# The last layer of a sixteen-batch perceiver moved into the attention in front of it, with three smaller edits

## The chip, the cores and the metric

The kernel runs on one core of one Trainium2 chip. The time is the device time of one execution in microseconds (us). A core has TensorE (PE; its weight loads are shown apart as PEld), VectorE (DVE), ScalarE (ACT), GpSimd (POOL) and SyncE (SP), which here issues all loads and stores. Each runs its own list of instructions in order; they meet through semaphores.

## The reference

Twelve sections run one after the other on x, a 16 x 64 x 256 array in float32: four layers, each with a cross-attention over a context of 16 x 1601 x 256, a self-attention and a feed-forward part. Each section adds its result to x after a layer norm of x. What matters here:

```
# layer 0, cross-attention (16 heads; k, v are the context): softmax over keys
attn = softmax(where(mask, min, q k^T / 4));  x += concat(attn v) w_o
# layer 2, cross-attention: relu(scores + bias)^2 on the unmasked keys,
# divided by its sum, times v;  x += (...) Wo^T
# layer 3, self-attention: softmax(q k^T / 4 + relative bias, causal), projection
# layer 3, feed-forward: one linear layer with 8-bit weights
xn = layernorm(x)
x_scale = max(abs(xn), axis=-1) / 127          # at least 1e-6 before the division
x_q = clip(round(xn / x_scale), -128, 127)
x += (x_q @ weight_q) * x_scale * weight_scale + bias
```

## The kernel before, in words

The 1024 tokens (16 batches of 64) are eight tiles of 128 (`NT = 8`), two batches to a tile; x stays in SBUF as `self.x`, 128 x 8 x 256, for the whole run. `run` calls the sections of `STAGES`; each opens its own pools of SBUF and PSUM, and its first instructions wait until the memory they reuse is free.

A layer that plans the order sits between the program text and the engines: instructions go to their engine in an order that it derives from its own costs, unless a section sets `self.pinned`. Then `mm` and `tr` (lines 2018 and 2023, which nearly all products and transposes share in the profile) keep TensorE's instructions in the order in which the program writes them.

**Setup** (line 57) loads three things on SP's queue: the constants `cst` (the identity among them), x in one transfer of 1 MB, and the small vectors `vecs`. The weights of the first section and the first context tiles `cT` follow. SP's transfers share eight semaphores in turn, so a transfer may wait for the landing of the one eight before it.

**The norm** (`layernorm`, line 122) takes statistics of all eight tiles on VectorE (lines 127, 128), one reciprocal root for all (`rstd`, line 112: VectorE, ScalarE's square root, VectorE) and then eight normalisations (line 131). `transpose` (line 135) turns pairs of tiles on TensorE into `xT`, and products such as `lin_t` (line 156) or `lin` (line 170) follow. Five sections used it: the cross-attentions of layers 0 and 2, the expert sections of layers 0 and 2, and the last feed-forward section.

**The streamed cross-attentions** of layers 0 and 2 (`stream`, line 1914) go through 16 batches of 13 chunks of 128 keys, two chunks at a time: keys and values are projected (`pk`), scores are taken by key (`sc`), ScalarE makes weights `e` of them, and `values` (line 1959) multiplies them with the values into `acc`. The sums of the weights are made elsewhere: `total` (line 1948) adds `e` of each chunk into `tot` on GpSimd (line 1957), and when a batch is done `finish_heads` (line 1862) multiplies `tot` with ones into the second half of `acc`, takes the reciprocal and writes the batch's columns of the heads. Then `lin` with `wo` projects the heads tile by tile and `add_to_x` (line 330) adds them to x.

**The self-attention of layer 3** (`token_attention`, line 2041) runs over tiles with the order of TensorE pinned. In step t: `scores(t)` (scores, bias and maximum on VectorE, subtraction of the maximum on GpSimd, line 2136, exponential on ScalarE), `values(t - 1)` (turn of the weights on TensorE, copies on ScalarE, products and sums into `acc`, reciprocal and product on VectorE, lines 2162 and 2163), `project(t - 2)` (product with `wo`, addition to x). The tile of scores `sc` has one buffer, `mm` has two, which turns and projections share.

**The feed-forward of layer 3** (`l3_ffn`, line 1820) then runs over all of x: norm, maximum (line 1833), scale, three instructions a tile for the rounding (lines 1842 to 1844, with the large constant `big`), transposes of the bf16 result, product with the weights, scaling (line 1856), bias on GpSimd (line 1857), addition to x (line 1858). `run` ends with one store of x (line 2212).

Of the kernel before, what the change touches and what calls it, by code (L numbers as in the profile page):

```python
# [19 lines left out]
P = 128  # L20
# [29 lines left out]
class Sections:  # L50
# [6 lines left out]
    def setup(self, ctx):  # L57
        nc, tc = self.nc, self.tc
        self.const = ctx.enter_context(tc.tile_pool(name="const", bufs=1))
        self.wp = ctx.enter_context(tc.tile_pool(name="weights", bufs=1))  # L60
        n = self.d["consts"].shape[1]
        self.cst = self.const.tile([P, n], F32, tag="cst", name="cst")
        nc.sync.dma_start(self.cst, self.d["consts"])
        self.x = self.const.tile([P, NT, D], F32, tag="x", name="x")
        nc.sync.dma_start(self.x, self.d["x"].rearrange("(t p) d -> p t d", p=P))
        n = self.d["vecs"].shape[1]
        self.vecs = self.const.tile([P, n], F32, tag="vecs", name="vecs")
        nc.sync.dma_start(self.vecs, self.d["vecs"])
        self.ident = self.c("ident")
        self.ss = self.const.tile([P, NT, NCH, 2], F32, tag="ss", name="ss")  # L70

# [49 lines left out]

    def layernorm(self, pool, src, dst, eps=1e-5):
        nc = self.nc
        mv = pool.tile([P, NT, 2], F32, tag="ln_mv", name="ln_mv")
        for t in range(NT):
            st = pool.tile([P, 6], F32, tag="ln_st", name="ln_st", bufs=3)
            nc.vector.bn_stats(st, src[:, t, :])
            nc.vector.bn_aggr(mv[:, t, :], st)
        r = self.rstd(pool, mv[:, :, 1], eps, "ln_r")
        for t in range(NT):  # L130
            nc.vector.tensor_scalar(
                dst[:, t, :], src[:, t, :], mv[:, t, 0:1], r[:, t : t + 1], ALU.subtract, ALU.mult
            )

    def transpose(self, ps, src, dst, scale=None, shift=None, tag="tr"):

# [47 lines left out]
    def l0_xattn(self):  # L184
        nc, tc, d = self.nc, self.tc, self.d
        with ExitStack() as ctx:
# [4 lines left out]
            wk = self.w2(d["L0_xattn_w_k"], "wk")  # L191
            wv = self.w2(d["L0_xattn_w_v"], "wv")
            wo = self.w2(d["L0_xattn_w_o"], "wo")
            xln = sb2.tile([P, NT, D], F32, tag="e", name="xln", bufs=3)
            xT = sb.tile([P, KC, T], F32, tag="xT", name="xT")
            qT = sb.tile([P, KC, T], F32, tag="qT", name="qT")
# [1585 lines left out]
    def l3_attn(self):  # L1782
        nc, tc, d = self.nc, self.tc, self.d
        with ExitStack() as ctx:
# [22 lines left out]
            for h in range(2):  # L1807
                o = slice(h * S, (h + 1) * S)
                for r in range(4):
                    keys = slice(16 * r, 16 * r + 16)  # L1810
                    of = pb[o, r, : 16 * H].rearrange("p (k g r h) -> p h g r k", g=2, r=4, h=2)[:, h]
                    for g in range(KC):
                        for j in range(2):
                            nc.vector.tensor_tensor(
                                bias[o, :, 2 * g + j, keys], of[:, g], above[o, :, keys].to_broadcast([S, 4, 16]), ALU.add)
            self.token_attention(sb, sb2, ps, w, wo, self.v("L3_attn_b_attn"), rows, 0.25, False, bias)

    def l3_ffn(self):
        nc, tc, d = self.nc, self.tc, self.d
        with ExitStack() as ctx:  # L1820
            sb = ctx.enter_context(tc.tile_pool(name="l3f", bufs=1))
            ps = ctx.enter_context(tc.tile_pool(name="l3f_ps", bufs=2, space=PSUM))
            w8 = sb.tile([P, KC, D // 4], I32, tag="w8i", name="w8i")
            nc.sync.dma_start(w8, d["L3_ffn_weight_q"].rearrange("(c p) n -> p c n", p=P))
            w = sb.tile([P, KC, D], BF16, tag="wb", name="wb")
            nc.vector.tensor_copy(w, w8.bitcast(mybir.dt.int8))
            rows = self.row(sb, "L3_ffn_weight_scale", "L3_ffn_bias")
            identb = sb.tile([P, P], BF16, tag="identb", name="identb")
            nc.vector.tensor_copy(identb, self.ident)
            xln = sb.tile([P, NT, D], F32, tag="xln", name="xln")  # L1830
            self.layernorm(sb, self.x, xln)
            am = sb.tile([P, NT], F32, tag="am", name="am")
            nc.vector.tensor_reduce(am, xln, AX.X, ALU.max, apply_absolute_value=True)
            xs = sb.tile([P, NT], F32, tag="xs", name="xs")
            nc.vector.tensor_scalar(xs, am, 1e-6, 1.0 / 127.0, ALU.max, ALU.mult)
            rx = sb.tile([P, NT], F32, tag="rx", name="rx")
            nc.vector.reciprocal(rx, xs)
            xq = sb.tile([P, NT, D], BF16, tag="xq", name="xq")
            big = 1.5 * 2.0**23
            for t in range(NT):  # L1840
                q = sb.tile([P, D], F32, tag="q", name="q", bufs=2)
                nc.vector.tensor_scalar(q, xln[:, t, :], rx[:, t : t + 1], big, ALU.mult, ALU.add)
                nc.vector.tensor_scalar(q, q, big, 127.0, ALU.subtract, ALU.min)
                nc.vector.tensor_scalar(xq[:, t, :], q, -128.0, None, ALU.max)
            xqT = sb.tile([P, KC, T], BF16, tag="xqT", name="xqT")
            for t in range(0, NT, 2):
                pt = ps.tile([P, KC, 2, P], BF16, tag="tr", name="trb")
                for c in range(KC):
                    for j in range(2):
                        nc.tensor.transpose(pt[:, c, j, :], xq[:, t + j, c * P : (c + 1) * P], identb)  # L1850
                for c in range(KC):
                    self.copy(xqT[:, c, t * P : (t + 2) * P], pt[:, c].rearrange("p j x -> p (j x)"))

            def evac(t, pm):
                y = sb.tile([P, D], F32, tag="y", name="y", bufs=2)
                nc.vector.scalar_tensor_tensor(y, pm, xs[:, t : t + 1], rows[:, 0:D], ALU.mult, ALU.mult)
                nc.gpsimd.tensor_tensor(y, y, rows[:, D : 2 * D], ALU.add)
                nc.vector.tensor_tensor(self.x[:, t, :], y, self.x[:, t, :], ALU.add)

            self.lin(ps, w, xqT, evac)  # L1860

    def finish_heads(self, sb2, hT, b, acc, totals, ones, eps=None):


        nc = self.nc
        for g in range(2):
            for j in range(4):
                self.mm(
                    acc[32 * j : 32 * j + 32, 2 + g, :], ones, totals[g][j], start=False, stop=True, skip_group_check=True
                )  # L1870
        rec = sb2.tile([P, 2, P], F32, tag="rec", name="rec")
        if eps is None:
            nc.vector.reciprocal(rec, acc[:, 2:4, :])
        else:
            nc.vector.tensor_scalar(rec, acc[:, 2:4, :], eps, None, ALU.add)
            nc.vector.reciprocal(rec, rec)
        half = sb2.tile([P, 2, 2, S], F32, tag="half", name="half")
        own = self.c("own2")
        for h in range(2):
            q = slice(h * S, (h + 1) * S)  # L1880
            nc.vector.scalar_tensor_tensor(
                half[:, h], acc[:, 0:2, q], own[:, h : h + 1], rec[:, :, q], ALU.mult, ALU.mult
            )
        nc.vector.tensor_tensor(hT[:, :, b * S : (b + 1) * S], half[:, 0], half[:, 1], ALU.add)
# [29 lines left out]
    def stream(self, ps, sb2, load, wk, wv, copy, weights, finish, extra=None):  # L1914
# [44 lines left out]
        def values(n):  # L1959
            x, c = xs[n // NCH], n % NCH  # L1960
            e = by_chunk(es[n // 2])[:, :, :, n % 2, :]
            if c == 0:
                x.acc = ps.tile([P, 4, P], F32, tag="acc", name="acc")
            total(x, c, e)
            w = min(P, SK - c * P)
            for g in range(2):
                for j in range(4):
                    self.mm(
                        x.acc[32 * j : 32 * j + 32, g, :], x.v[:w, c, (4 * g + j) * 32 : (4 * g + j + 1) * 32],
                        e[:w, j, 2 * g : 2 * g + 2, :], start=(c == 0 and g == 0), stop=(c == NCH - 1),  # L1970
                        skip_group_check=True,
                    )
# [65 lines left out]
                        junk, piece[:, c - lo, :], AF.Square, accum_out=self.ss[:, b // 2, c, b % 2 : b % 2 + 1])  # L2038
                    yield

    def token_attention(self, sb, sb2, ps, w, wo, bias_t, rows, scale, own_input, bias=None):

# [128 lines left out]
        for _ in linear(0):  # L2173
            pass
        rest = linear(1)
        es = {}
        for t in range(NT + 2):
            if t < NT:
                es[t] = scores(t)
            for _ in range((3, 3, 2, 2)[t] if t < 4 else 0):  # L2180
                next(rest)
            if t == 3:
                next(rest, None)
            if 0 < t <= NT:
                values(t - 1, es.pop(t - 1))
            if t > 1:
                project(t - 2)
        self.pinned = False

    def l3_load(self, t, kind):  # L2190
# [3 lines left out]
        for j in range(2):  # L2194
# [5 lines left out]
            else:  # L2200
# [1 line left out]
            self.loaded[kind, t, j] = x  # L2202

    STAGES = ["l0_xattn", "l0_attn", "l0_ffn", "l1_xattn", "l1_attn", "l1_ffn",
              "l2_xattn", "l2_attn", "l2_ffn", "l3_xattn", "l3_attn", "l3_ffn"]

    def run(self, stages):
        with ExitStack() as ctx:
            self.setup(ctx)
            for s in stages:  # L2210
                getattr(self, s)()
            self.nc.sync.dma_start(self.out.rearrange("(t p) d -> p t d", p=P), self.x)

# [138 lines left out]
```

## Time and profile before

| what | us |
|---|---|
| median of three runs | 3904.95 (3902.84 to 3907.98) |
| the profiled execution, its own time | 3893.54 |
| its span | 3891.7 |
| TensorE busy in the span | 3541.6 |
| VectorE busy in the span | 1994.1 |
| ScalarE busy in the span | 1402.5 |
| GpSimd busy in the span | 1339.2 |
| first transpose of TensorE starts at | 12.44 |
| first streamed attention's last projection ends at about | 873.7 |
| layer 2's streamed attention's last projection ends at about | 3130.8 |
| last feed-forward section, first instruction of its norm at | 3857.41 |
| store of x issued at | 3885.88 |

The profile is of one execution on the chip; all starts are counted from the start of its span. A line of the timeline gives the start, the length, the engine, the line of the kernel, the operation, what it writes and reads, and in brackets how long the engine had been idle and what ended that. A busy TensorE is not one at its full pace; the granted clock says how much of the pace it was given.

### The profile page before, as it was taken

Reading aid. Unit: us, or ns where it says so; the run is one execution under the profiler, and the core shown is the slowest. Engines: PE = TensorE matmul, PEld = TensorE weight load, DVE = VectorE, ACT = ScalarE, POOL = GpSimd, SP = SyncE. Lnnn points to the kernel's source line nnn. Section 1 sums busy time; section 2 is a strip of 40 time slices with the busy share of each in tenths; the row PEclk is TensorE's granted clock in tenths of the full one; section 3 lists DMA queues with packets and bytes.
Section 4 is the critical chain, followed back from the end, with each engine's and each line's share of the span. In section 5 each row is a group of like instructions: output and inputs, shape, how many; then the busy total and the mean of one; then the engine's idle time right before and its main releaser. Section 6 shows DMA issues by size and latency. Waiting matters only on the chain.

```text
span 3891.7 us, 70627 instructions
## 1 busy us (share of the span) xinstructions
PE 3541.6 (91%) x30986; PEld 2238.7 (58%) x30986; DVE 1994.1 (51%) x3623; ACT 1402.5 (36%) x1955; POOL 1339.2 (34%) x767
## 2 busy tenths in 40 slices
PE   8999999988899988999997899899999879999985
PEld 4555555555565555555554566567676646555453
DVE  4333334335454445565656564567776656333346
ACT  2333333336411111444432433266666622111212
POOL 1555555562221101243331110377777740000011
PEclk9999999998999979999998999999999989999987
DMA  3111111006300004323400000211111004111640
GB/s 122 37 37 37 37 37 37 19 21 211 125 28 30 22 17 147 105 98 114 141 20 23 22 1 6 90 54 37 54 37 54 2 10 166 35 41 30 258 182 16
DMA packets 97212, 248.83 MB, mean 64 GB/s; under 512 B 7764, under 2 KB 68831, under 8 KB 94728
## 3 DMA queue, kind: packets, MB, share of 16 engines
q1 hardware_dynamic: 96904, 244.31, 17.6%
q8 instruction: 243, 3.98, 0.4%
q14 instruction: 65, 0.53, 0.0%
HBM read 243.24 MB, written 1.05 MB: 63 GB/s over the span
## 4 chain that ended last, share of the span: by engine, by line
PE 56%; DVE 10%; ACT 3%; issue 2%; POOL 1%; DMA 1%; SPq 0%; DVEq 0%; POOLq 0%; ACTq 0%
PE pk L2018 8%; PE sc L2018 7%; PE lin L177 5%; PE pu L2018 3%; PE gate L1619 3%; PE up L1619 3%; PE acc L2018 3%; PE pc L1246 3%; PE lin L442 2%; PE prz L2018 2%; PE lin_t L432 2%; PE lin_t L164 2%; PE gelu_t L1156 2%; PE turn L2023 1%; PE lin L2018 1%
## 5 line engine op out<-in xcount | busy, mean ns | idle before, releaser
L1957 POOL TENSOR_TENSOR tot<-tot,e 128x1024 f32<-128x1024 f32 (+1 forms) x352 | 831.3, 2362 | 377.3 <-ACT e L304 251.1
L247 DVE TENSOR_REDUCE m<-sc 128x4 f32<-128x2048 f32 x96 | 220.1, 2292 | 271.8 <-PE sc L2018 270.7
L1386 DVE SCALAR_TENSOR_TENSOR e<-sc,row_L_xattn_nbias,free 128x2048 f32<-128x2048 f32 x104 | 244.3, 2349 | 123.6 <-PE sc L2018 116.2
L1388 ACT ACTIVATE e<-e 128x2048 f32<-128x2048 f32 x104 | 198.6, 1910 | 244.7 <-DVE e L1386 244.7
L304 ACT ACTIVATE e<-sc 128x2048 f32<-128x2048 f32 x104 | 195.2, 1877 | 240.7 <-PE sc L2018 235.7
L2018 PE MATMUL sc<-qb,kT 32*128 32x128 f32 x6656 | 246.4, 285 | 38.5 <-DVE m L261 12.4
L2018 PEld LDWEIGHTS sc<-qb,kT 32*128 32x128 f32 x6656 | 207.3, 188 | 84.2 <-issue 24.9
L2018 PE MATMUL acc<-e,v 128*32 128x128 f32 x6656 | 229.0, 279 | 8.8 <-ACT e L1389 8.8
L2018 PEld LDWEIGHTS acc<-e,v 128*32 128x32 f32 x6656 | 171.9, 111 | 109.8 <-issue 96.3
L2018 PE MATMUL pk<-cT,wk 128*128 128x512 f32 (+1 forms) x512 | 208.0, 534 | 3.6 <-DVE rows L277 3.6
L2018 PE MATMUL pk<-wv,cT 128*128 128x256 f32 x832 | 208.6, 393 | 0.0
L1389 ACT ACTIVATE e<-e 128x2048 f32<-128x2048 f32 x104 | 198.8, 1911 | 3.3
L2018 PE MATMUL pk<-cT,wkv 128*128 128x512 f32 (+1 forms) x512 | 196.3, 524 | 0.0
L2018 PE MATMUL pk<-wkv,cT 128*128 128x256 f32 x832 | 196.3, 386 | 0.0
L2018 PEld LDWEIGHTS pk<-wv,cT 128*128 128x128 f32 x832 | 149.2, 189 | 75.3 <-issue 57.2
L2018 PEld LDWEIGHTS pk<-wkv,cT 128*128 128x128 f32 x832 | 153.2, 190 | 28.4 <-issue 4.3
L791 POOL TENSOR_TENSOR e<-e,mx 128x512 f32<-128x512 f32 x96 | 81.6, 882 | 214.0 <-DVE mx L790 214.0
L1246 PE MATMUL pc<-ew,eh 128*128 128x256 f32 x640 | 155.1, 385 | 0.0
L2018 PE MATMUL sc<-kT,qb 32*128 32x512 f32 (+2 forms) x1536 | 139.3, 460 | 12.2 <-issue 1.0
L2018 PE MATMUL pu<-cn,e 128*64 128x257 f32 (+1 forms) x1248 | 143.0, 385 | 5.6 <-POOL e L801 5.6
L1623 ACT ACTIVATE g<-gate 128x512 f32<-128x512 f32 x68 | 40.6, 597 | 294.6 <-PE gate L1619 294.6
L2018 PE MATMUL sc<-cT,qT 128*64 128x512 f32 (+1 forms) x768 | 142.3, 519 | 1.9 <-DMA cT<-in_ctx_t 1.3
(476 smaller groups left out, 6371.9 us busy)
## 6 DMA issues: line engine op xcount, KB each, us to landing
cT<-in_ctx_t SPq DMA_DIRECT2D x128, 832.0 KB
cn<-in_ctx_n SPq DMA_DIRECT2D x32, 1664.0 KB
piece<-in_ctx_n SPq DMA_DIRECT2D x16, 896.0 KB
piece<-in_ctx_n SPq DMA_DIRECT2D x16, 768.0 KB
w<-in_L_attn_W SPq DMA_DIRECT2D x8, 1024.0 KB
w<-in_L_ffn_W SPq DMA_DIRECT2D x16, 256.0 KB
down<-in_L_ffn_w_down SPq DMA_DIRECT2D x16, 256.0 KB
gate<-in_L_ffn_w_gate SPq DMA_DIRECT2D x16, 256.0 KB
```

What stands on the lines that cost most here:

```text
L164: nc.tensor.matmul(pm, w[:, k, n * P : (n + 1) * P], xT[:, k, h * 512 : (h + 1) * 512], start=(k == 0), stop=(k == kc - 1),)
L177: nc.tensor.matmul(pm, xT[:, k, t * P : (t + 1) * P], w[:, k, :], start=(k == 0), stop=(k == kc - 1))
L247: nc.vector.tensor_reduce(x.m4[:, g, :, i], pm, AX.X, ALU.max)
L304: nc.scalar.activation(e, pm, AF.Exp, scale=0.25)
L791: pin(nc.gpsimd.tensor_tensor(p.e, p.e, p.mx.unsqueeze(2).to_broadcast(p.shape), ALU.subtract))
L1246: nc.tensor.matmul(pc[:, n, j, :], s.eh[i][:, c, tok], ew2[:, c, cols], start=False, stop=(c == 3))
L1386: nc.vector.scalar_tensor_tensor(e16, pm16, nb, free[:, at : at + P].unsqueeze(1).to_broadcast([P, 16, P]), ALU.add, ALU.mult)
L1388: nc.scalar.activation(e, e, AF.Relu)
L1389: nc.scalar.activation(e, e, AF.Square)
L1619: nc.tensor.matmul(pm[-1], w[:, k, n * P : (n + 1) * P], xT[:, k, tok], start=(k == 0), stop=(k == KC - 1))
L1957: nc.gpsimd.tensor_tensor(tot[:w], x.first if c == 1 else tot[:w], e[:w], ALU.add)
L2018: ins = self.nc.tensor.matmul(*args, **kw)
```

## The change

Four edits. Setup loads x by two tiles, with the constants behind the first load and the vectors behind the first section's weights. `layernorm` works on two tiles at a time, each pair with its own root. In `stream`, the last batch's chunks 7 to 12 no longer go through GpSimd: TensorE multiplies `e` itself with ones (`add_sums`) beside the products with the values. And `l3_ffn` is no section of its own: it returns an object whose parts `token_attention` calls. After `project` of tiles 1, 3, 5, 6 and 7, `prepare` normalises and quantises the tiles that have become ready; in later steps `turn` transposes one of them in front of the attention's `values`, and `product` follows behind it and stores the tile. The rounding takes two VectorE instructions and one of ScalarE, the bias is added to x beforehand on GpSimd, and the copies of the transposes are ScalarE's. TensorE's order stays pinned throughout.

```diff
         self.cst = self.const.tile([P, n], F32, tag="cst", name="cst")
-        nc.sync.dma_start(self.cst, self.d["consts"])
         self.x = self.const.tile([P, NT, D], F32, tag="x", name="x")
-        nc.sync.dma_start(self.x, self.d["x"].rearrange("(t p) d -> p t d", p=P))
+        for t in range(0, NT, 2):
+            nc.sync.dma_start(self.x[:, t : t + 2], self.d["x"][t * P : (t + 2) * P].rearrange("(t p) d -> p t d", p=P))
+            if t == 0:
+                nc.sync.dma_start(self.cst, self.d["consts"])
...
     def layernorm(self, pool, src, dst, eps=1e-5):
         nc = self.nc
-        mv = pool.tile([P, NT, 2], F32, tag="ln_mv", name="ln_mv")
-        for t in range(NT):
-            st = pool.tile([P, 6], F32, tag="ln_st", name="ln_st", bufs=3)
-            nc.vector.bn_stats(st, src[:, t, :])
-            nc.vector.bn_aggr(mv[:, t, :], st)
-        r = self.rstd(pool, mv[:, :, 1], eps, "ln_r")
...
+        for t0 in range(0, NT, 2):
+            mv = pool.tile([P, 2, 2], F32, tag="ln_mv", name="ln_mv", bufs=2)
+            for j in range(2):
+                st = pool.tile([P, 6], F32, tag="ln_st", name="ln_st", bufs=3)
+                nc.vector.bn_stats(st, src[:, t0 + j, :])
+                nc.vector.bn_aggr(mv[:, j, :], st)
+            r = self.rstd(pool, mv[:, :, 1], eps, f"ln_r{t0}")
...
+            groups = {1: [0, 1], 3: [2, 3], 5: [4, 5], 6: [6], 7: [7]}
+            def prepare(s, us):
...
+                r = self.rstd(sb2, mv[:, :n, 1], 1e-5, "f_r")
+                xln = sb2.tile([P, 2, D], F32, tag="f_x", name="f_x")
+                for j, t in enumerate(us):
+                    nc.vector.tensor_scalar(
+                        xln[:, j, :], self.x[:, t, :], mv[:, j, 0:1], r[:, j : j + 1], ALU.subtract, ALU.mult)
+                am = sb2.tile([P, 2], F32, tag="f_am", name="f_am")
+                nc.vector.tensor_reduce(am[:, :n], xln[:, :n], AX.X, ALU.max, apply_absolute_value=True)
...
+                for j, t in enumerate(us):
+                    q = sb2.tile([P, D], F32, tag="f_q", name="f_q")
+                    nc.vector.tensor_scalar(q, xln[:, j, :], rx[:, j : j + 1], big, ALU.mult, ALU.add)
+                    nc.vector.tensor_scalar(q, q, big + 127.0, big - 128.0, ALU.min, ALU.max)
+                    xq[t] = sb2.tile([P, D], BF16, tag="f_xq", name="f_xq", bufs=4)
+                    nc.scalar.activation(xq[t], q, AF.Identity, bias=less)
+                    nc.gpsimd.tensor_tensor(self.x[:, t, :], self.x[:, t, :], rows[:, D : 2 * D], ALU.add)
+                    xs[t] = sc[:, j : j + 1]
+            def turn(s, t):
+                pt = ps.tile([P, KC, P], BF16, tag="mm", name="trb", bufs=2, padded_shape=[P, KC, 512])
                 for c in range(KC):
+                    self.tr(pt[:, c, :], xq[t][:, c * P : (c + 1) * P], identb)
+                xq[t] = sb2.tile([P, KC, P], BF16, tag="f_qT", name="f_qT")
+                nc.scalar.copy(xq[t], pt)
+            def product(s, t):
+                pm = ps.tile([P, D], F32, tag="mm", name="f_lin", bufs=2, padded_shape=[P, 512])
...
+                y = sb2.tile([P, D], F32, tag="f_y", name="f_y")
+                nc.vector.scalar_tensor_tensor(y, pm, xs[t], rows[:, 0:D], ALU.mult, ALU.mult)
                 nc.vector.tensor_tensor(self.x[:, t, :], y, self.x[:, t, :], ALU.add)
+                nc.sync.dma_start(self.out[t * P : (t + 1) * P, :], self.x[:, t, :])
...
+    def add_sums(self, acc, weights, w):
+        for g in range(2):
             for j in range(4):
                 self.mm(
+                    acc[32 * j : 32 * j + 32, 2 + g, :], self.c("ones")[:w, :32], weights[g][j], start=False, stop=True,
+                    skip_group_check=True)
...
-            total(x, c, e)
             w = min(P, SK - c * P)
+            if x.b < B - 1 or c < 7:
+                total(x, c, e)
+            else:
+                self.add_sums(x.acc, [[e[:w, j, 2 * g : 2 * g + 2, :] for j in range(4)] for g in range(2)], w)
...
+            now = ready[:1]
+            for u in now:
+                then.turn(u)
             if 0 < t <= NT:
                 values(t - 1, es.pop(t - 1))
+            for u in now:
+                then.product(u)
+                ready.remove(u)
             if t > 1:
                 project(t - 2)
+                if then is not None and t - 2 in then.groups:
+                    us = then.groups[t - 2]
+                    then.prepare(us)
+                    ready += us
+        for u in ready:
+            then.turn(u)
+        for u in ready:
+            then.product(u)
...
-            self.nc.sync.dma_start(self.out.rearrange("(t p) d -> p t d", p=P), self.x)
```

## The prediction

> **What bounds the kernel now.** I read the page first: TensorE is busy for 91% of the span, so most of the time can only be moved by an edit that takes TensorE work away, and this change takes none (it adds some). What it can win lies where TensorE stands still.
>
> ```profile
> span 3891.7 us, 70627 instructions
> PE 3541.6 (91%) x30986; PEld 2238.7 (58%) x30986; DVE 1994.1 (51%) x3623; ACT 1402.5 (36%) x1955; POOL 1339.2 (34%) x767
> ```
>
> Then the timeline around each place that the diff touches (columns: start, length, engine, line, operation, shape; in brackets the idle time before and what ended it). First, the end of the first streamed attention:
>
> ```profile
> 843.59 21.77 POOL L1957 TENSOR_TENSOR tot<-tot,e 128x1024 f32<-128x1024 f32 x9
> 853.46 1.08 PE L2018 MATMUL acc<-e,v 128*32 128x128 f32 x32
> 865.42 1.08 PE L2018 MATMUL acc<-tot,cst 128*32 128x128 f32 x16 [9.82 <-POOL tot L1957]
> 874.79 0.17 DVE L117 TENSOR_SCALAR ln_r<-ln_mv 128x4 f32<-128x4 f32 x1
> ```
>
> The last product with values ends at 854.5, but GpSimd is nine sums of 2.4 us behind, and TensorE waits until 865.4. In the windows view the granted clock of 865.4 to 877 is 0.65, so the last projections run slowly too. Layer 2's streamed attention ends the same way, with a shorter wait:
>
> ```profile
> 3120.18 1.08 PE L2018 MATMUL acc<-e,v 128*32 128x128 f32 x32
> 3124.28 0.64 PE L2018 MATMUL acc<-tot,cst 128*32 128x128 f32 x16 [2.40 <-POOL tot L1957]
> 3128.71 2.08 PE L177 MATMUL lin<-wo,xT 128*128 128x256 f32 x4 [3.15 <-DVE xT L1884]
> ```
>
> At the start TensorE waits for the norm of all eight tiles, which waits for one load of x:
>
> ```profile
> 7.93 0.75 DVE L127 BATCH_NORM_STATS2 ln_st<-x 128x6 f32<-128x256 f32 x2 [2.86 <-DMA x<-in_x]
> 12.44 2.08 PE L143 MATMUL tr<-cst,xln 128*128 128x128 f32 x8 [12.44 <-DVE xln L131]
> 17.73 7.03 PE L164 MATMUL lin_t<-xT,wq 128*128 128x512 f32 x16
> ```
>
> At the end the chain of waits is VectorE after the attention's last product (3855.7): 34.4 us, of which VectorE is busy 24.0, then one store. Before it the loop over tiles takes about 5.7 us a tile, with VectorE busy 22.2 of 31.3 us in the windows view.
>
> ```profile
> 3829.43 1.90 POOL L2136 TENSOR_TENSOR e<-e,mx 128x1024 f32<-128x1024 f32 x1 [8.98 <-DVE mx L2135]
> 3829.59 1.76 DVE L2162 RECIPROCAL rec<-acc 128x256 f32<-128x256 f32 x1 [0.33 <-PE acc L2018]
> 3861.33 1.28 ACT L118 ACT_TABLE_LOAD   x1 [9.37 <-DVE ln_r L117]
> 3885.88 0.40 SPq L2212 DMA_DIRECT2D out<-x  x1
> ```
>
> **Part 1, sums by ones (first stream).** For the last batch's chunks 7 to 12 GpSimd loses six sums of 2.36 us; TensorE gets six times eight products of the form of acc<-e,v. That row is 229.0 us for 6656 records, two to a product, so a chunk costs 0.54 us and all six 3.3. In the loop of 3.44 us around 850 the new 1.08 us per pair of chunks takes the place of one projection (1.13), which moves behind. GpSimd then ends at about 865.4 - 6 x 2.42 = 850.9, so its part is no longer waited for. From 853.46: sums and products 2.1, GpSimd's part 0.54: 856.1. Seven projections follow; the first two are paced by their additions behind the 1.76 us reciprocal in VectorE's order (until about 860), the others at 1.13. The norm of the next layer's first half needs tiles up to 5 and is queued behind them: 863.8, against 874.79 now. After it come the additions of tiles 6 and 7, which the table load (1.28) about covers. I take 10.5 us. Bounds: 13.5 if the additions don't pace the projections, 3 if GpSimd is still behind.
>
> **Part 1, second such stream.** Products and sums end at 3119.4 + 2.2 = 3121.6, GpSimd's part at 3122.1, then 0.42 + 1.74 + 0.6 + 0.3 with gaps to 3125.45, the last projection 1.1 warm and its addition 0.4: 3127.0, against 3131.24 now: 4.2 us. Bounds 2 and 6.
>
> **Part 2, start.** x comes in four loads, the constants behind the first, the vectors behind the weights. Three loads more on SP's queue, each 0.4 to 0.5 us of issue; the context loads there also wait for earlier loads of the ring (cT waited 1.9 us for x). They come later by some 2 us, but the queue stays full (348 GB/s until 24.6), and TensorE now asks for cT after lin_t instead of at 14.3, so nothing waits. The last pair still lands near 7.9. The statistics of pair 3 wait for that load, and pair 2's normalisation is queued behind them; this and pair 3's remainder take VectorE about 3.8 us, and TensorE's last transposes end near 12.2; lin_t starts there instead of 17.7, but the two context products (1.85 + 1.02) that ran before it now come after: 12.2 + 7.0 + 1.7 = 21.0 against 24.59, if TensorE is warm. The first 3.5 us of work ran at half pace (eight transposes 2.08, later eight 1.04). Sparse transposes may leave it so: 1.7 less. I take 3.0; bounds 1.5 and 4.5.
>
> **Part 3, norms by two tiles elsewhere.** VectorE gets six small instructions more (0.17 and 0.20 each), but TensorE's first transpose comes earlier: 1378.92 to about 1376.9, and the half-clocked 11 us of work behind it pull the gate's end from 1390.7 to about 1388.5: 2.0. In layer 2's expert stage 3241.18 to about 3240.0: 1.0. In the streamed attention of that layer the table load stays in front: 0.7. Bounds together 1 and 6.
>
> **Part 4, last layer inside the attention.** Gone from the end: all of 3857.3 to 3891.7 but the last tile's part. What is left after the last projection's addition: two single-tile norms and quantisations interleaved, 18 VectorE instructions, 5.3 us by the rows (0.17 to 0.40 each); then ACT 0.37, transposes 0.35, copy 0.42, product 0.6, scaling and addition 1.35; then the store. The old store's issue to the end took 5.8, of which its 1.05 MB moved for 3.0 us; a tile's is an eighth: 3.2. In all 11.7, so 22.7 won.
>
> Against it, the loop. TensorE's order is fixed there, and a tile's transposes stand in front of the attention's own turn. They need the whole quantisation of a pair, and that starts only when the second tile's addition is done. Behind these transposes wait, on the same queue, the turn of the attention's tile, its acc, both projections and the next scores, and VectorE's reciprocal waits for acc. (The eight stores wait on SP's queue with nothing but stores behind them.) Take the pair (0, 1), from its addition at 3825.98: hT and statistics to 3826.75; e and mx of tile 4, ahead in VectorE's order, 2.65: 3829.4. Now GpSimd's subtraction of tile 4 starts, 1.9 us. Then root 0.8, two normalisations 0.67, maximum 0.6, small ones 0.44, q 0.62 and 0.28, ACT 0.4, transposes 0.35, turn 0.66, copies 1.2, acc 1.35.
>
> Here a rule speaks against the change. The row: normalisations of this kind take 1.38 for four, but
>
> ```profile
> 3606.46 1.38 DVE L1662 TENSOR_SCALAR xln<-x,ln_mv,ln_r 128x256 f32<-128x256 f32 x4
> 3608.15 2.34 POOL L1668 TENSOR_TENSOR x<-x,row_L_xattn_bv 128x1024 f32<-128x1024 f32 x1 [371.90 <-PE tr L2023]
> 3609.00 2.62 DVE L1662 TENSOR_SCALAR xln<-x,ln_mv,ln_r 128x256 f32<-128x256 f32 x4 [0.17 <-PE tr L2023]
> ```
>
> the second four stand until GpSimd's operation is over. The Trainium skill, "SBUF — State Buffer", "Who interferes with whom": such a VectorE instruction and a GpSimd one lock each other out for the whole instruction. So the normalisations wait until 3831.45, and the small ones behind GpSimd's two new additions of the bias (0.7 each, L1857). The reciprocal of tile 3 (3829.59) comes at about 3839.0: 9.5 late. The pair (2, 3) has a statistic between mx and its root, so the root itself is locked out: 12.2 more. The pair (4, 5) meets no subtraction: 7.4 more. Sum 29.1. Behind the last reciprocal (3853.22, 38.5 us before the end) there are then about 17.9. Net 29.1 - 20.6 = 8.5 us slower. Without the lock the same walk gives 23.7 - 21.3 = 2.4 slower; if the queueing on TensorE cost nothing and only VectorE's added 3.1 us a tile counted, against 9 us idle there, 11 faster. I take 7 slower, near the locked walk, as its row is in this trace; range -11 to +12.
>
> Table loads: four more. The trace shows 1.28 and the root 0.01 later; "ScalarE: Activation LUTs", "What ACT_TABLE_LOAD costs", gives 2.66 with its drain. By the trace all fall into idle time of ACT; by the page the third root would come 1 us later. I follow the trace: 0. The weights' loads move from 3857 to before the loop: their 0.64 us of casts fall into VectorE's idle time there.
>
> **Sum.** -10.5 - 4.2 - 3.0 - 2.0 - 1.0 - 0.7 + 7 = -14.4. The profiled run took 3893.54 (span 3891.7), so 3879.1 for it; the median of the three runs is 11.4 above it, so 3904.95 - 14.4 = 3890.5.
>
> **Rivals.**
> - The last layer hides well after all (-11): 3872.5. For it: ACT and GpSimd are idle enough; against: the fixed TensorE order. 0.2.
> - GpSimd still gates the first stream's end (gain 3 instead of 10.5): 3898. For: it is busy 14.1 of 14.6 us before 854.6; against: six sums are 14 us. 0.1.
> - The start gains nothing, as the context loads come later than 19 us: 3893.5. For: SP's queue waits for landings; against: 13 us is when the first landed. 0.1.
> - Slower: the transposes in TensorE's order, from a cost of 29 us in the loop beyond what the end saves, 12 to 13 a pair more than walked: it would take every one of the quantisation's VectorE instructions being locked out. 3915. 0.05.
>
> **How the numbers follow.** My forecast 0.55. 0.2% is 7.8 us, about what this measurement tells from no change. Faster: 0.55 + 0.2 + 0.1 and half of the second rival, less the forecast's upper edge: 0.85; same 0.11; slower 0.04. The range runs from the first rival to the second: 3873 to 3899.
>
> **What would show it.** Right: no wait for tot before the last acc<-tot; lin_t near 12; rec of tile 7 some 25 to 29 us later relative to the stage's start and the end some 18 us behind it; f_x or f_r of 1 to 2 us beside GpSimd. Wrong: a loop that still takes 6 us a tile, or a TensorE gap near 856.

## The result, and the profile after

| kernel | median us | range | runs |
|---|---|---|---|
| before | 3904.95 | 3901.50 to 3910.06 | 5 |
| changed | 3890.39 | 3883.65 to 3895.43 | 5 |

The ratio is 0.9966, with a 95% interval of 0.9952 to 0.9980: 13 us less, between 8 and 19. The forecast was 3890.5. So the total was met almost to the microsecond, but not because every term was right, as the stretches show.

The page of the changed kernel, first lines:

```profile
span 3893.4 us, 71039 instructions
PE 3559.3 (91%) x31163; PEld 2254.0 (58%) x31178; DVE 2001.7 (51%) x3655; ACT 1415.8 (36%) x1987; POOL 1311.5 (34%) x756
```

This profiled execution took 3895.43 us, 1.9 more than the profiled one of before (3893.54), although the medians differ by 14.6 the other way: executions of one kernel scatter by some 10 us to either side of their median, and the one profiled of before was among the fastest of its kernel. Subtracting one span from the other would therefore say "no gain". What can be compared is each stretch between two instructions that both kernels have: the difference of the two starts, followed through the trace, shows where time is won and lost. It also shows a difference that no forecast named. In layer 2's self-attention, from about 3190 us of the trace of before to its end at about 3230, no instruction differs, and yet the changed kernel takes 7 us more there. The windows view of the same work, before and then after (columns: window, its length, the busy time and count of the five engines, granted clock, DMA share, GB/s):

```profile
3192.30:3212.30 20.00, 16.83 (x271) 12.79 (x270) 11.32 (x20) 4.92 (x4) 9.57 (x2) 0.83 0.01 2
3212.30:3232.30 20.00, 18.46 (x396) 15.29 (x398) 18.91 (x33) 0.00 (x0) 1.16 (x1) 0.91 0.01 2
```

```profile
3180.00:3200.00 20.00, 17.16 (x175) 13.02 (x175) 8.30 (x14) 4.92 (x4) 5.33 (x1) 0.63 0.01 2
3200.00:3220.00 20.00, 19.25 (x346) 16.20 (x346) 15.10 (x25) 0.00 (x0) 5.39 (x2) 0.69 0.01 2
```

The granted clock is 0.83 and 0.91 in the one, 0.63 and 0.69 in the other, and in the same 40 us TensorE gets through 667 products there, 521 here. Every later trace of this study has this stretch 4.4 to 7.3 us longer than the one of before, among them a kernel with nothing but part 1 changed (5.8). The work that takes 22.0 us there from 3190 on, at a granted clock of 0.84, takes 27.5 to 28.7 us at 0.63 in all ten. It may belong to the execution, for the one that was traced of before was 11 us faster than the median. But that kernel was traced only once, and all ten other traces hold part 1, so no run here excludes that it follows from the change. The stretches below leave it out.

Now the places that were forecast. The end of the first streamed attention, in the timeline of the changed kernel (start, length, engine, line, operation, shape, and in brackets the idle time before):

```profile
840.04 12.12 POOL L1986 TENSOR_TENSOR tot<-tot,e 128x1024 f32<-128x1024 f32 x5
856.11 0.62 PE L2050 MATMUL acc<-e,v 65*32 65x128 f32 x16
856.55 0.62 PE L2050 MATMUL acc<-tot,cst 128*32 128x128 f32 x16
863.68 0.17 DVE L118 TENSOR_SCALAR ln_r<-ln_mv 128x4 f32<-128x4 f32 x1
```

GpSimd ends at 852.2, TensorE takes its part at 856.55 with no idle time in front (9.82 us before), and the next norm's root begins at 863.68; the forecast had 863.8.

The start, same view:

```profile
7.22 1.23 PE L145 MATMUL tr<-cst,xln 128*128 128x128 f32 x4 [7.22 <-DVE xln L133]
11.63 1.98 PE L145 MATMUL tr<-cst,xln 128*128 128x128 f32 x8 [1.44 <-ACT xT L111]
13.67 9.12 PE L166 MATMUL lin_t<-xT,wq 128*128 128x512 f32 x16
22.62 5.31 PE L2050 MATMUL pk<-cT,wk 128*128 128x512 f32 x12
27.86 1.14 PE L2050 MATMUL sc<-kT,qb 32*128 32x512 f32 x8
```

The first transpose comes 5.2 us earlier than before, but the first scores (27.86) only 0.26 us earlier: lin_t, 7.03 us before, now takes 9.12.

And the end. Before and after in the windows view, from the reciprocal of tile 2 to that of tile 7, and from there to the end:

```profile
3823.70:3853.20 29.50, 24.29 (x829) 18.70 (x829) 21.62 (x23) 9.69 (x14) 7.60 (x4) 0.97 0.01 3
3853.20:3891.70 38.50, 8.47 (x40) 4.76 (x40) 26.82 (x79) 2.88 (x6) 5.61 (x8) 0.58 0.12 37
```

```profile
3822.00:3878.20 56.20, 31.06 (x847) 24.09 (x848) 38.99 (x75) 20.30 (x32) 12.02 (x10) 0.71 0.04 12
3878.20:3893.40 15.20, 4.63 (x22) 2.18 (x20) 10.15 (x32) 2.42 (x7) 1.44 (x2) 0.72 0.10 35
```

The last reciprocal is 26.7 us later against tile 2's, the end stands 15.2 behind it instead of 38.5: 68.0 us have become 71.4. The timeline says what holds the loop:

```profile
3828.11 1.99 DVE L1852 TENSOR_SCALAR f_x<-x,f_mv,f_r 128x256 f32<-128x256 f32 x2
3832.16 0.49 DVE L1863 TENSOR_SCALAR f_q<-f_q 128x256 f32<-128x256 f32 x2
3833.05 0.40 PE L2055 MATMUL trb<-identb,f_xq 128*128 128x128 bf16 x2 [8.17 <-ACT f_xq L1865]
3833.24 1.92 PE L2055 MATMUL turn<-cst,e 128*128 128x128 f32 x8
3837.47 1.76 DVE L2195 RECIPROCAL rec<-acc 128x256 f32<-128x256 f32 x1 [4.82 <-PE acc L2050]
```

TensorE stands idle for 8.17 us in front of trb, although the weights for the turn behind it have been ready since 3830.7. VectorE, which could do the attention's reciprocal, then waits 4.82 us for acc. The same pattern comes again at 3854.81 and 3873.74.

The table collects the stretches. "Measured" is the mean over all traces of this study that have the part, less the mean over those that don't; for the ends of the two streams that is the one trace of before, and for the start the two kernels with products of zeros (see below) are left out. In times of the trace of before, the first six rows run from 0 to 28.1 us, 848 to 882, 1341 to 1388, 2440 to 2477, 3060 to 3150 and 3232 to 3252.

| stretch | forecast | measured | the traces, as differences from the one of before |
|---|---|---|---|
| start, to the first scores | -3.0 | -0.8 | -1.5 to +0.6 with, -0.4 to +0.9 without |
| end of the first stream | -10.5 | -11.3 | -11.0 to -11.5 in ten traces |
| norm of layer 0's experts | -2.0 | -2.5 | -2.1 to -3.1 with, -0.2 to 0 without |
| norm in layer 2's stream | -0.7 | +0.3 | +0.1 to +3.3 with, 0 to +1.9 without |
| end of layer 2's stream | -4.2 | -2.0 | -3.0 to -4.5 in six traces, -0.6 to +1.1 in four |
| norm of layer 2's experts | -1.0 | -0.4 | -0.1 to +0.7 with, 0 to +1.2 without |
| last layer (tile 2's reciprocal to the end) | +7 | +2.6 | in full: 71.1 to 71.5 with, 68.0 to 69.4 without |
| sum | -14.4 | -14.1 | |

If the longer self-attention of layer 2 (6 us in the mean) belonged to part 1, the sum would be about -8, at the edge of the measured 8 to 19.

### The profile page after: what moved, and what is told of

It reads as the page before. It is cut to its first block, busy times and chain, and to the rows that moved or that the text cites. A ratio compares the mean times of both kernels' runs of the same rounds, so it can differ in the third digit from the quotient of the medians.

```text
span 3893.4 us, 71039 instructions
## 1 busy us (share of the span) xinstructions
PE 3559.3 (91%) x31163; PEld 2254.0 (58%) x31178; DVE 2001.7 (51%) x3655; ACT 1415.8 (36%) x1987; POOL 1311.5 (34%) x756
## 4 chain that ended last, share of the span: by engine, by line
PE 55%; DVE 10%; ACT 3%; issue 2%; POOL 1%; DMA 1%; DVEq 0%; ACTq 0%; SPq 0%; POOLq 0%
PE pk L2050 9%; PE sc L2050 7%; PE lin L179 5%; PE pu L2050 3%; PE acc L2050 3%; PE gate L1622 3%; PE up L1622 3%; PE pc L1249 3%; PE prz L2050 2%; PE lin_t L166 2%; PE lin L445 2%; PE turn L2055 1%; PE gelu_t L1159 1%; PE lin_t L435 1%; PE lin L2050 1%
## 5 line engine op out<-in xcount | busy, mean ns | idle before, releaser
L1986 POOL TENSOR_TENSOR tot<-tot,e 128x1024 f32<-128x1024 f32 (+1 forms) x340 | 803.0, 2362 | 375.0 <-ACT e L307 252.2
```

The source lines that it names most:

```text
L1986: nc.gpsimd.tensor_tensor(tot[:w], x.first if c == 1 else tot[:w], e[:w], ALU.add)
```

## The experiments

Times in one group were taken on one chip, with the kernel before beside them (medians 3903.65, 3903.95 and 3903.76 in the three groups).

### First group: what each part is worth, and what the end waits for

The last layer put back into a section of its own, with `l3_ffn` as in the kernel before:

```diff
-                ..., rows, 0.25, False, bias, self.l3_ffn(sb, sb2, ps))
+                ..., rows, 0.25, False, bias)
-    def l3_ffn(self, sb, sb2, ps):
...
+    def l3_ffn(self):
...
-              "l2_xattn", "l2_attn", "l2_ffn", "l3_xattn", "l3_attn"]
+              "l2_xattn", "l2_attn", "l2_ffn", "l3_xattn", "l3_attn", "l3_ffn"]
```

> The changed kernel, but the last layer stands in its own section behind the attention as before, with its maximum over all tiles, three-instruction rounding and one store (its norm goes by two tiles, as the shared function now does). My theory (the move into the attention costs about 7 us, as TensorE's fixed order makes the attention wait for the quantisation): the last reciprocal of the attention comes some 27 us earlier and the end 38 us behind it instead of 15, so 3890.4 - 7 = about 3883 to 3887. The rival (the last layer hides well, and the gain comes from it): about 3901.

Measured: 3889.78 (3881.91 to 3894.12), ratio 0.9967 (0.9955 to 0.9979), above the 3883 to 3887 of my theory. The total is level with the changed kernel's 0.9966, and intervals of some 5 us to either side settle neither theory beyond saying that the gain doesn't come from this part, since 3901 is excluded. The stretch settles the sign: 30.9 us between the two reciprocals and 37.7 behind, 68.7 against 71.4. The move costs 2 to 3 us, not 7.

The turn one step later:

```diff
-            now = ready[:1]
+            now = [u for u in ready[:1] if t > since[u] + 1]
...
                     ready += us
+                    since.update((u, t) for u in us)
```

> The changed kernel, but a prepared tile is transposed one step later than now, so that TensorE no longer waits for the quantisation in front of the attention's own turn. My theory (most of the 26.7 us by which the last reciprocal comes late is this wait): the reciprocal of tile 3 comes at its old place, the last one 8 to 14 us late instead of 26.7, the end 15 to 17 behind it: about 3874 to 3879. The rival (VectorE's added work, 3 us a tile, and its lock-out by GpSimd are the price, wherever the transposes stand): the last reciprocal stays over 20 us late, 3884 or more.

Measured: 3888.79 (3885.98 to 3893.45), ratio 0.9966 (0.9954 to 0.9978). The time is where the rival had it (3884 or more); the last reciprocal, 18.0 us late, lies between the 8 to 14 of my theory and the rival's 20. The trace tells why:

```profile
3827.69 1.76 DVE L2195 RECIPROCAL rec<-acc 128x256 f32<-128x256 f32 x1 [0.25 <-PE acc L2050]
3835.40 0.40 PE L2055 MATMUL trb<-identb,f_xq 128*128 128x128 bf16 x2 [5.63 <-ACT f_xq L1865]
3841.61 1.76 DVE L2195 RECIPROCAL rec<-acc 128x256 f32<-128x256 f32 x1 [6.52 <-PE acc L2050]
```

Tile 3's reciprocal is back in its old place (5.8 us behind tile 2's), as expected. But VectorE now takes the reciprocal and the next tile's maximum first, the quantisation ends only at 3835.7, and the transposes wait for it all the same, with tile 4's turn behind them. The wait was shortened and moved by a tile, not removed: 47.5 us between the reciprocals, 66.3 to the end. My expectation forgot that a later place in TensorE's order also lets VectorE do the quantisation later.

TensorE kept busy at the start:

```diff
-                    nc.tensor.transpose(pt[:, c, j, :], src[:, t + j, c * P : (c + 1) * P], self.ident)
+                    ins = nc.tensor.transpose(pt[:, c, j, :], src[:, t + j, c * P : (c + 1) * P], self.ident)
+                    if warm:
+                        self.tc.keep_in_program_order(ins)
+            for _ in range(warm[2] if warm else 0):
+                self.tc.keep_in_program_order(
+                    nc.tensor.matmul(warm[0], warm[1][:, :P], warm[1], start=True, stop=True))
...
+            for _ in range(14):
+                self.tc.keep_in_program_order(
+                    nc.tensor.matmul(idle, warm[:, :P], warm, start=True, stop=True))
             self.layernorm(sb, self.x, xln)
-            self.transpose(ps, xln, xT, tag="acc")
+            self.transpose(ps, xln, xT, tag="acc", warm=(idle, warm, 6))
```

These transposes and the products of zeros also keep the program's order on TensorE.

> The changed kernel, with 14 products of zeros (bf16, 128x512, into an unused PSUM tile) on TensorE before the first transposes and 6 behind each pair of tiles; their result is not used. My theory (the start gained only 0.3 us instead of 3.0, because TensorE ran the transposes and the first part of lin_t at half pace: 9.12 us against 7.03 before): lin_t takes about 7.0, the context's products after it begin about 2 to 3 us earlier than 22.6, and the kernel gains 2 to 3 us: about 3888. The rival (the late end of the transposes, 13.6, is what counts, or the loads): lin_t still takes 9, or the products wait for cT and wk, gain under 0.5.

Measured: 3897.77 (3888.46 to 3901.87), ratio 0.9983 (0.9974 to 0.9991).

```profile
1.19 5.86 PE L218 MATMUL idle<-warm 128*128 128x512 bf16 x14 [1.19 <-DVE warm L214]
13.62 0.60 PE L145 MATMUL tr<-cst,xln 128*128 128x128 f32 x4
14.05 1.46 PE L150 MATMUL idle<-warm 128*128 128x512 bf16 x5
15.35 7.03 PE L171 MATMUL lin_t<-xT,wq 128*128 128x512 f32 x16
```

lin_t takes 7.03, so the half pace was the cause of its 9.12; but the products of zeros behind the last pair hold it back by 1.5 us, so that the first scores come 0.4 us earlier than in the changed kernel, not 2 to 3. The total is even above the changed kernel's. Behind the start VectorE, ScalarE and GpSimd have the same order in both, and the excess arises in stretches whose code is the same. I can't tell its cause, and it didn't come again with the smaller warming below.

Part 1 alone, on the kernel before:

```diff
-            total(x, c, e)
             w = min(P, SK - c * P)
+            if x.b < B - 1 or c < 7:
+                total(x, c, e)
+            else:
+                self.add_sums(x.acc, [[e[:w, j, 2 * g : 2 * g + 2, :] for j in range(4)] for g in range(2)], w)
```

> The kernel before with one part of the change alone: the last batch's chunks 7 to 12 summed on TensorE by ones, in both streams. My theory: the end of the first stream comes 10 to 12 us earlier, that of layer 2's stream 4 us, so 3904.95 - 15 = about 3890. The rival (GpSimd is still behind): an idle time of TensorE before acc<-tot is left, 3898 to 3902.

Measured: 3895.07 (3890.71 to 3899.77), ratio 0.9980 (0.9969 to 0.9992): 3 to 12 us faster, below what I expected.

```profile
855.74 0.62 PE L2024 MATMUL acc<-e,v 65*32 65x128 f32 x16
856.17 0.62 PE L2024 MATMUL acc<-tot,cst 128*32 128x128 f32 x16
863.30 0.17 DVE L117 TENSOR_SCALAR ln_r<-ln_mv 128x4 f32<-128x4 f32 x1
```

No idle time is left before acc<-tot, so GpSimd isn't behind, and the stretch gives 11.4 us in the first stream and 3.5 at the end of the second, together 14.9 as expected. The time of whole runs shows only a part of it: its interval ends at 12. What takes the rest isn't known. The longer self-attention of layer 2, 5.8 us in this trace too, would be of the right size.

### Second group: the turn behind the attention

The changed kernel again, as its companion:

> The changed kernel unaltered, beside the next two on one chip. Both theories: about 3890 in time, and the last layer's stretch (from layer 3's attention's first row load to the end) some 5 to 7 us longer than in the kernel before.

Measured: 3887.88 (3880.85 to 3895.13), ratio 0.9963 (0.9950 to 0.9975); 71.3 us from tile 2's reciprocal to the end. From the first row load of layer 3's attention to the end it takes 4.1 us longer than before, less than the 5 to 7 expected; in the first trace of the changed kernel it is 6.8, of which 3.4 lie in front of tile 2's reciprocal.

Then the order that the trace of the turn one step later asks for. Nothing of the last layer stands in front of the attention's work of a step:

```diff
-            now = ready[:1]
-            for u in now:
-                then.turn(u)
+            for u in turned:
+                then.product(u)
             if 0 < t <= NT:
                 values(t - 1, es.pop(t - 1))
-            for u in now:
-                then.product(u)
-                ready.remove(u)
             if t > 1:
                 project(t - 2)
+                turned = [u for u in ready[:1] if t > since[u] + 1]
+                for u in turned:
+                    then.turn(u)
+                    ready.remove(u)
...
+                    since.update((u, t) for u in us)
+        for u in turned:
+            then.product(u)
         for u in ready:
```

> The changed kernel, but in each step a prepared tile is transposed behind the attention's turn, products and projection, no sooner than two steps after its preparation, and its product with the weights follows in the next step. My theory (TensorE's fixed order is the price: in the changed kernel and in the one with the turn a step later, the attention waited at the transposes until the quantisation was done): from the reciprocal of tile 2 to that of tile 7 about 40 us instead of 56.2 (29.5 before), from there to the end about 17, so that the stretch from tile 2's reciprocal to the end is 55 to 60 instead of 71.4 (68.0 before): 3874 to 3879. The rival (VectorE's added work is the price, wherever the transposes stand): 65 or more for this stretch, 3885 or more.

Measured: 3875.47 (3866.93 to 3882.14), ratio 0.9930 (0.9912 to 0.9948), 12.4 us below its companion.

```profile
3827.48 0.73 DVE L1852 TENSOR_SCALAR f_x<-x,f_mv,f_r 128x256 f32<-128x256 f32 x2
3833.17 0.28 PE L2055 MATMUL trb<-identb,f_xq 128*128 128x128 bf16 x2 [0.72 <-ACT f_xq L1865]
3848.07 1.72 DVE L1882 TENSOR_TENSOR x<-f_y,x 128x256 f32<-128x256 f32 x1
```

```profile
3819.60:3858.60 39.00, 29.80 (x844) 22.70 (x844) 34.87 (x72) 19.36 (x30) 12.67 (x10) 0.85 0.04 13
3858.60:3874.50 15.90, 4.92 (x26) 2.52 (x24) 10.90 (x35) 3.78 (x11) 1.48 (x2) 0.71 0.12 41
```

trb now costs TensorE 0.72 us of waiting instead of 8.17. 39.0 us lie between the reciprocals and 15.9 behind, 54.9 together: 16.4 less than the changed kernel, 13.1 less than the kernel before. VectorE is busy 34.87 of the 39.0 us, so here it is near its bound; in the changed kernel it was busy 39.0 of 56.2. The rival, that VectorE's added work is the price wherever the transposes stand, has fallen: it gave 65 or more. To the end, VectorE's busy time fell too, from 49.1 to 45.8 us, as fewer of its instructions run beside GpSimd's (f_x takes 0.73 in the first line, not 1.99). So up to 3.4 of the 16.4 us may come from that.

Parts 2 and 3 undone: setup and `layernorm` as in the kernel before, all else as changed.

> The changed kernel with x loaded in one transfer behind the constants and all norms by eight tiles, as before (parts 2 and 3 undone). From the two traces: the start within 0.5 us of the changed kernel's, the expert section of layer 0 some 3 us later, of layer 2 1 us later, the streamed attention of layer 2 1 to 2 us earlier: together 2 to 3.5 us slower, 3893. My forecast on record had 6.7 for these parts; if that holds, 3897.

Measured: 3891.24 (3881.77 to 3902.95, 22 runs), ratio 0.9971 (0.9964 to 0.9979), 3.4 us above its companion. The intervals overlap, but the stretches of parts 2 and 3 give 0.8 + 2.6 = 3.4 as well: the two parts are worth about that, not the 6.7 on record. In its trace the experts' norms cost 3.1 and 1.3 us more than in the changed kernel's, as expected; layer 2's stream, which was to come 1 to 2 us earlier, takes 0.6 more.

### Third group: a start that is warm and not held up

The kernel with the turn behind the attention, and the 14 products of zeros at the start; behind the pairs of tiles there are fewer than in the first try:

```diff
-            for _ in range(warm[2] if warm else 0):
+            for _ in range(warm[2][t // 2] if warm else 0):
...
-            self.transpose(ps, xln, xT, tag="acc", warm=(idle, warm, 6))
+            self.transpose(ps, xln, xT, tag="acc", warm=(idle, warm, (4, 4, 2, 0)))
```

> The kernel with the turn behind the attention, and TensorE warmed at the start with 14 products of zeros before the first transposes, 4, 4 and 2 behind the first three pairs and none behind the last (in the run before 6 stood behind each pair, and those behind the last held lin_t back by 1.5 us). My theory: lin_t starts near 13.8 and takes 7.0, so the products with the context behind it begin at about 20.8 instead of 22.6: 1.5 to 2 us faster than the same kernel without, about 3873. The rival (TensorE falls back to half pace in the gaps between the transposes, or the context loads land later than that): no gain.

> The kernel with the turn behind the attention once more, beside the one with the warm start: 3875, with 54 to 56 us from tile 2's reciprocal to the end.

Measured: with it 3871.29 (3861.72 to 3876.95), ratio 0.9915 (0.9901 to 0.9930); without, again, 3875.58 (3870.80 to 3885.71), ratio 0.9929 (0.9915 to 0.9943). The starts, with and then without:

```profile
1.19 5.39 PE L218 MATMUL idle<-warm 128*128 128x512 bf16 x14 [1.19 <-DVE warm L214]
13.41 7.13 PE L171 MATMUL lin_t<-xT,wq 128*128 128x512 f32 x16 [0.19 <-ACT xT L111]
20.39 5.31 PE L2061 MATMUL pk<-cT,wk 128*128 128x512 f32 x12
25.63 1.14 PE L2061 MATMUL sc<-kT,qb 32*128 32x512 f32 x8
```

```profile
13.58 8.18 PE L166 MATMUL lin_t<-xT,wq 128*128 128x512 f32 x16
21.59 5.31 PE L2050 MATMUL pk<-cT,wk 128*128 128x512 f32 x12
26.84 1.14 PE L2050 MATMUL sc<-kT,qb 32*128 32x512 f32 x8
```

The first scores come at 25.63 against 26.84 in this pair (27.86 in the changed kernel's first trace), and no other line of the two kernels differs. The totals differ by 4.3 us, with overlapping intervals; the start accounts for 1.2 of it here, and for 0.9 to 2.2 against the other traces whose first transposes begin at the same time to 0.1 us. The kernel with the warm start has the lowest median of the study, 0.85% below the one before (0.70% to 0.99%). From tile 2's reciprocal to the end both take 54.9 us.

## Why the prediction was right, and where it wasn't

**Part 1, first stream: right.** Each step of it held: GpSimd out of the way (852.2 against 850.9), sums and products until about 857, projections paced by their additions, root at 863.7. The measured 11.3 lies 0.8 above the value taken. That the root met the forecast to 0.1 us is luck in part: the whole loop stands 1.3 us later in this trace, and counted from it the root comes 12.4 us earlier than before, in all ten traces, not 11.0. About 1 us is lost again in the next section, where a root's VectorE instruction runs beside a GpSimd addition and takes 1.28 us, before 0.48.

**Part 1, second stream: right where it says what happens, too large on average.** The wait for tot is gone in all traces. In six of ten the stretch is 3.0 to 4.5 us shorter, as forecast; in the other four the 20 us in front of this end ran at a lower granted clock (0.65 to 0.72, against 0.75 to 0.83 in the six), and nothing of the gain is seen against the one trace of before. Whether the kernel before loses there as well in such executions was not traced.

**Part 2, start: wrong, below its bounds.** The failed step is "if TensorE is warm". The forecast named the other case ("Sparse transposes may leave it so: 1.7 less") and took 3.0 with bounds of 1.5 to 4.5; it measured 2.1 less by lin_t alone (9.12 against 7.03 in the profile; 7.9 to 9.1 in five others). The rest is lin_t's start, 13.67 instead of 12.2: the copies that free the transposes' two buffers stood in VectorE's order behind the next pairs' statistics, so the third pair's transposes began at 11.63, released by a copy, and not by their norm. lin_t's products stand 0.85 us apart until 17.2, and 0.43 from 17.9 on. The Trainium skill, "TensorE: Matmul & The Clock Gate", "What's actually happening", says that TensorE is at half pace until it has been busy for about 3.4 us on end. The 14 products of zeros show that very step: 0.43 us apart until 5.4, that is for 4.2 us, and 0.216 after. That rule applied to transposes of 1.2 us with gaps between them speaks for the cold lin_t; the forecast's own figure for it leaves 3.0 - 1.7 = 1.3 us for the start, and the measured 2.1 leaves 0.9.

**Part 3: the sum 2.6 against 3.7 forecast.** Layer 0's experts as forecast and slightly more, layer 2's 0.6 less. The larger miss is the norm inside layer 2's stream (+0.3 instead of -0.7). GpSimd builds its mask there, and the normalisations run into it. The first line is the kernel before, the others the changed one:

```profile
2468.67 3.85 DVE L131 TENSOR_SCALAR xln<-x,ln_mv,ln_r 128x256 f32<-128x256 f32 x8
2455.95 2.50 DVE L133 TENSOR_SCALAR xln<-x,ln_mv,ln_r 128x256 f32<-128x256 f32 x4
2456.36 1.95 POOL L1362 TENSOR_SCALAR free<-m 128x832 uint8<-128x832 uint8 x2 [4.38 <-DVE xln L133]
2459.53 1.90 DVE L133 TENSOR_SCALAR xln<-x,ln_mv,ln_r 128x256 f32<-128x256 f32 x2
```

Two alone take 0.73, so four took about 1.1 us too long and the next two 1.2. I had weighed the mutual exclusion of VectorE and GpSimd for the last layer only. But it is not the whole cause: eight took 3.85 before, where eight alone take 2.67, so one collision was there already; the second one comes in only two of the eight traces with pairs, and the two with the greatest loss (+3.3 and +3.2) don't have it. What costs them their time stays open.

**Part 4: sign and mechanism right, size off by 4.4.** That the transposes in TensorE's fixed order make the attention wait was the heart of the walk, and the order behind the attention, which takes away no instruction and moves only the transposes and the product, gives back 16.4 us. The walk's first pair was exact: the reciprocal of tile 3 came 9.6 us late (9.5 forecast). The mis-sized terms are two. The pair (2, 3) was to cost 12.2, because its root would be locked out by GpSimd; its root began at 3849.44, 0.05 us ahead of GpSimd's subtraction, so the pair cost 9.9 (the third: 7.0, forecast 7.4):

```profile
3849.44 0.17 DVE L118 TENSOR_SCALAR f_r<-f_mv 128x2 f32<-128x2 f32 x1
3849.49 1.90 POOL L2169 TENSOR_TENSOR e<-e,mx 128x1024 f32<-128x1024 f32 x1 [4.31 <-DVE f_mv L1848]
3850.08 1.78 DVE L1852 TENSOR_SCALAR f_x<-x,f_mv,f_r 128x256 f32<-128x256 f32 x2
3870.07 0.73 DVE L1852 TENSOR_SCALAR f_x<-x,f_mv,f_r 128x256 f32<-128x256 f32 x2
```

That makes 26.7 instead of 29.1. And behind the last reciprocal there are 15.2 us instead of 17.9: 10.7 instead of 11.7 behind the last projection's addition, and 4.5 instead of 6.2 in front of it. The whole is +3.4 against the one trace and +2.6 against the mean of three. That this lies near the 2.4 of the walk without the lock is chance: in the first trace the loop lost 3.0 us more than that walk gave, and the end saved 2.0 more. The reading of the lock itself holds: f_x took 1.99 and 1.78 for two beside GpSimd's subtraction, and 0.73 where GpSimd had finished. The Trainium skill, "SBUF — State Buffer", "Who interferes with whom", adds that an instruction with two inputs from SBUF is locked out too, beside a GpSimd one that reads SBUF; the last line of the first fence of the turn behind the attention shows it, an addition of 0.42 us that took 1.72 beside GpSimd.

**Rivals.** "The last layer hides well" was wrong for this order of TensorE and right for another: the order behind the attention ends 13 us earlier than the kernel before in that stretch, beyond the 11 that it was given. "GpSimd still gates" is excluded by the trace. "The start gains nothing" came nearest to the truth, but through TensorE's pace, not through late loads. "Slower" by the transposes was the right mechanism; its threshold was not reached. That threshold was summed wrongly: a net cost of 29 us is 20.5 above the walk's 8.5, some 7 us a pair, not 12 to 13.

**The sum.** -14.4 was forecast and -14.1 is the sum of the stretches. That they agree is luck, because errors of both signs met: the start, the end of layer 2's stream and that layer's two norms fell short by 6.0 together, while the last layer cost 4.4 less and two other stretches gave 1.3 more. The median of whole runs is no finer test, as its interval is 5 us to either side.

## What to carry to other kernels

When work is woven into a loop whose engine order is fixed by hand, place it behind the loop's own instructions of the step and late enough for its data: here the same instructions cost 2.6 us in front and won 13 behind. Read a gain of a few tenths of a per cent stretch by stretch, against more than one trace, before believing a difference of two spans. An earlier start of TensorE is worth little if its first products are too sparse to bring it to full pace; a few products of zeros while the loads run did that here (7.13 us for lin_t instead of 8.18), though the time of whole runs doesn't show it clear of their scatter.

## What was not expected of the hardware

The text ahead of the prediction says that the granted clock tells how much of the pace TensorE was given. It doesn't tell all: the half pace after idleness doesn't show in it. In the window of lin_t it stands at 1.00, while products at first take twice as long:

```profile
13.60:22.60 9.00, 8.94 (x17) 3.94 (x17) 1.81 (x3) 0.97 (x3) 0.72 (x2) 1.00 1.04 392
```

A clock of 1.00 in a row is thus no sign that TensorE ran at full pace; the spacing of its products is. And stretches with the same code differ by up to 7 us between traces with different granted clocks, which is more than most of the parts of this change are worth; what sets that clock, no run here shows.
